# Layer 0 of a four-layer convolution and scan network: naming ScalarE's exp-and-ln table, and one silu visit for x and z

## The chip, the cores and the metric

The kernel runs on one core of a Trainium2 chip. The metric is device microseconds (us) for one execution of the whole program. A core has five engines that run side by side, each through its own queue in order: TensorE (PE, matrix products), VectorE (DVE), ScalarE (ACT, activation functions), GpSimd (POOL) and SyncE (SP, which here issues the DMA transfers).

ScalarE computes an activation function from a table that must be loaded first. `Silu`, `Exp` and `Ln` do not all lie in one table, so the program holds table loads (`ACT_TABLE_LOAD` in the profile) among ScalarE's work.

## The reference

Four layers run one after the other on an input of 2 x 128 channels x 64 x 64. Only layer 0 is touched. It is a layer norm over the channels, then a Mamba block run in four directions over the 4096 positions (rows forward and backward, columns forward and backward), then a projection of the four results and a residual sum. Cut to what matters:

```python
xz = x @ W_in.T
xh, z = split(xz, 2)
xc = causal_conv(xh, conv_w, width=4) + conv_b
xh = silu(xc)
dt, Bm, Cm = split(xh @ W_xp.T)
dt = softplus(dt @ W_dt.T + b_dt)          # exp and ln
dA = exp(dt[..., None] * A)                # A = -exp(A_log), 16 states
dBu = dt[..., None] * Bm * xh[..., None]
h = scan(h = dA * h + dBu)                 # along the positions
y = sum_over_states(h * Cm) + xh * Dp
y = y * silu(z)
return y @ W_out.T
```

The softplus is computed as `max(p, 0) + ln(1 + exp(-|p|))`, so layer 0 needs silu, exp and ln.

## The kernel before, in words

Layer 0 works through 64 chunks of 512 positions: two batch items, two orders (rows, columns), two directions (`rev` false, then true), and eight chunks in each. A chunk has 256 inner channels times 16 states, which are 32 groups of 128 rows. Two groups share one pass, so a chunk has **16 steps**, and step `s` of a chunk contains scan `s` on VectorE.

For one step, ScalarE makes `da = exp(dt * A)` into PSUM (`s_da`, line 396, two halves of 512 columns), GpSimd makes `dbu` (`s_dbu`, line 383), ScalarE corrects one column of `dbu` for the state carried over from the chunk before (`s_fix`, line 411), VectorE scans (`s_scan`, line 427), and the result is multiplied by C on VectorE (`s_hc`, line 439) or, in 5 of 16 steps, on GpSimd (line 437). TensorE sums the states (`s_y`, line 450). There are two `da` buffers in PSUM and three `dbu` buffers. So `da` of step s+1 waits for scan s-1, and `dbu` of step s+2 waits for scan s-1.

Everything is in an order written out by hand (`manual_schedule`): the loop from line 611 issues, in each step `s`, `s_dbu` of step s+2, scan `s`, VectorE's extra work `V[s]`, `s_hc` of step s-1, GpSimd's extra work `G[s]`, the sums `s_y` that are due, `s_da`, `s_fix` of step s+1 and `s_hst` of step s-1 on ScalarE, ScalarE's extra work `A[s]`, and TensorE's extra work `M[s]`. The dictionaries `A`, `V`, `M`, `G` prepare the next two chunks, `new` (the next) and `nxt` (the one after it):

- softplus for `new`: `M[0]`, `M[1]` and `A[1]`, `A[2]` (abs, `e_exp`, line 350), `A[3]` (`e_ln`, line 353), `V[5]`, `V[6]` (`dt_`, line 359), then `G[7]`, `G[8]` (`dtu_`, line 367).
- z for `new`, in the forward directions only: `pz(0)` and `pz(1)` on TensorE (line 294), each copied out by ScalarE with `z_` (line 300). They stand at `M[6]`, `A[7]` and `M[13]`, `A[14]`. `zsilu` (line 308) takes silu of both halves and stores the gate to DRAM, at `A[8]` of the chunk itself. The backward directions load the stored gate instead (`zload`).
- x for `nxt`: `px(0)` and `px(1)` (line 281, four products each) at `M[9]` and `M[10]`, copied out with `x_` (line 290) at `A[10]` and `A[12]`, then `xsilu` (line 304) at `A[13]`, `pd` (line 320) at `M[15]`.
- the layer norm of later positions in 12 chunks (`Norm0`; 0 to 3 and 15 to 22): `center` at `M[12]`, `sub` at `V[13]` (line 214), `square` at `A[14]`, `var` at `M[14]`; in the chunk after that `ln` and `exp` at `A[3]` (lines 232 and 235), `scale` at `M[7]`, `mul` at `V[8]`.

All the small products `pt`, `pz`, `px`, `pd`, `center`, `scale`, `var` and `po` pass through one PSUM buffer named `misc`. Each therefore waits until the engine that reads the one before it is done.

## Time and profile before

| what | value |
|---|---|
| three timed runs | 6545.72, 6548.74, 6561.89 us; median 6548.74 |
| profiled execution, first to last instruction (span) | 6564.3 us; no other time of that execution is recorded |
| first to last scan of layer 0 | 57.4 to 3464.2 us, 64 chunks, 53.2 us a chunk |
| busy over the span | PE 5817.9, DVE 5628.5, POOL 5420.7, ACT 4487.8 us |
| `ACT_TABLE_LOAD` | 1283 ns each |

The page prints the engines' busy shares, the span in 40 slices, the chain of work that ended last, and the costliest groups of instructions. In a line of the trace's timeline the columns are the start (us), the duration (us), the engine, the line of the kernel, the operation, what is written and read with shapes, the number of instructions merged into the row, and in brackets the idle time of the engine before it and what ended that idle time. Instructions of one engine overlap a little at their ends, so busy times are unions of intervals.

### The profile page before, as it was taken

How to read it: one execution, taken by the hardware profiler on the slowest of the kernel's cores; microseconds unless marked ns; L12 is line 12 of the kernel's file. 1: busy time of each engine (PE TensorE's matmuls, PEld its weight loads, DVE VectorE, ACT ScalarE, POOL GpSimd, SP SyncE). 2: the span in 40 equal slices, each digit the busy share in tenths (PEclk: the TensorE clock that was granted, in tenths of full speed). 3: DMA queues.
4: the chain of work that ended last, by engine and by line, in shares of the span. 5: the costliest groups of instructions: out<-in, count | busy, mean ns of one | idle time of the engine just before them, and what ended most of it. 6: DMA issues, size and time to landing. Idle time of an engine off the chain costs nothing. (4 is left out here: it accounts for less than half of the span.)

```text
span 6564.3 us, 66618 instructions
## 1 busy us (share of the span) xinstructions
PE 5817.9 (89%) x20014; PEld 2781.5 (42%) x20014; DVE 5628.5 (86%) x4540; ACT 4487.8 (68%) x7771; POOL 5420.7 (83%) x2543
## 2 busy tenths in 40 slices
PE   8888888888888888888888999999999999898888
PEld 2222222222222222222226888888888788222221
DVE  7999999999999999999997766666666766899997
ACT  7887778877788777887766665555556565555453
POOL 6999999999999999999995666655666566788886
PEclk7888777877788777887779999999999999889897
DMA  6566656566666666556650000000000000877775
GB/s 181 145 156 161 161 142 146 146 150 148 152 155 151 153 152 152 146 146 152 151 137 19 2 4 3 1 1 1 1 1 1 2 6 7 205 173 179 181 180 121
DMA packets 400476, 700.36 MB, mean 107 GB/s; under 512 B 74089, under 2 KB 76658, under 8 KB 399730
## 3 DMA queue, kind: packets, MB, share of 16 engines
q1 hardware_dynamic: 399232, 694.33, 43.3%
q8 instruction: 157, 2.57, 0.2%
q14 instruction: 205, 1.68, 0.1%
q10 hardware_dynamic: 882, 1.78, 0.1%
HBM read 584.53 MB, written 111.28 MB: 106 GB/s over the span
## 5 line engine op out<-in xcount | busy, mean ns | idle before, releaser
L383 POOL TENSOR_TENSOR dbu<-dus,bs 128x1024 f32<-128x1024 f32 x1024 | 2448.1, 2440 | 116.9 <-DVE h L427 98.8
L427 DVE TENSOR_TENSOR_SCAN h<-da,hst,dbu 128x1024 f32<-128x1024 f32 x896 | 2090.9, 2340 | 86.1 <-ACT dbu L411 80.7
L396 ACT ACTIVATE da<-dts,aneg 128x512 f32<-128x512 f32 (+1 forms) x2048 | 1410.1, 689 | 357.1 <-DVE h L427 318.9
L1004 POOL TENSOR_TENSOR sum<-sum,sc 128x1024 f32<-128x1024 f32 x378 | 898.1, 2376 | 504.1 <-ACT sc L999 500.4
L966 ACT COPY sc<-s 128x512 f32<-128x512 f32 x1024 | 596.9, 585 | 767.8 <-PE s L961 639.2
L961 PE MATMUL s<-q,k 128*128 128x256 f32 x4096 | 1053.8, 380 | 9.7 <-ACT lo L919 5.5
L1016 PE MATMUL av<-sc,v 128*128 128x256 f32 x4096 | 1051.2, 380 | 9.1 <-ACT sc L999 9.1
L450 PE MATMUL y<-hc,cst 128*32 128x512 f32 x4096 | 880.4, 753 | 200.2 <-DVE hc L439 186.6
L973 DVE TENSOR_TENSOR mx<-mx,s 128x512 f32<-128x512 f32 x896 | 609.3, 680 | 452.5 <-ACT sc L966 449.2
L439 DVE TENSOR_TENSOR hc<-h,pc 128x1024 f32<-128x1024 f32 x704 | 841.9, 1196 | 9.5 <-PE y L450 7.4
L961 PEld LDWEIGHTS s<-q,k 128*128 128x128 f32 x4096 | 777.0, 191 | 126.9 <-issue 8.8
L1016 PEld LDWEIGHTS av<-sc,v 128*128 128x128 f32 x4096 | 768.0, 190 | 112.9 <-ACT sc L999 14.1
L437 POOL TENSOR_TENSOR hc<-h,cs 128x1024 f32<-128x1024 f32 x320 | 770.0, 2406 | 1.2 <-issue 1.2
L416 PE MATMUL pc<-xd,sel 16*128 16x512 f32 x1024 | 707.0, 780 | 0.2
L1407 POOL TENSOR_TENSOR A<-A,D 128x1024 f32<-128x1024 f32 x224 | 526.9, 2370 | 138.8 <-DVE D L1412 102.1
L996 DVE TENSOR_TENSOR sc<-sc,pm 128x1024 f32<-128x1024 f32 x512 | 620.5, 1212 | 0.9 <-PE pm L992 0.9
L999 ACT ACTIVATE sc<-sc 128x1024 f32<-128x1024 f32 x512 | 541.8, 1058 | 41.2 <-DVE sc L996 41.0
L450 PEld LDWEIGHTS y<-hc,cst 128*32 128x32 f32 x4096 | 125.9, 120 | 858.3 <-DVE hc L439 427.6
L340 PE MATMUL misc<-xd,w_dt 9*128 9x512 f32 x504 | 364.6, 810 | 128.1 <-ACT x L479 68.5
L411 ACT ACTIVATE dbu<-hst,dbu,df 128x1 f32<-128x1 f32 x896 | 337.6, 377 | 65.3 <-POOL dbu L383 42.7
L1424 PE MATMUL q<-xs,room 32*128 32x512 f32 x840 | 291.1, 706 | 63.1 <-DVE A L1430 62.1
L416 PEld LDWEIGHTS pc<-xd,sel 16*128 16x128 f32 x1024 | 181.6, 218 | 350.2 <-issue 296.8
(315 smaller groups left out, 7792.9 us busy)
## 6 DMA issues: line engine op xcount, KB each, us to landing
dts<-ddt SPq DMA_DIRECT2D x512, 256.0 KB, 5.4
dus<-ddu SPq DMA_DIRECT2D x512, 256.0 KB, 5.1
D<-rows SPq DMA_DIRECT2D x448, 256.0 KB, 6.0
bs<-rows SPq DMA_DIRECT2D x1024, 64.0 KB, 4.9
cs<-rows SPq DMA_DIRECT2D x1024, 64.0 KB, 3.2
ddt<-dt SPq DMA_DIRECT2D x128, 256.0 KB, 2.0
ddu<-dtu SPq DMA_DIRECT2D x128, 256.0 KB, 4.0
dtr<-ddt SPq DMA_DIRECT2D x448, 64.0 KB, 2.0
```

Of the source, the lines that this page charges most:

```text
L383: nc.gpsimd.tensor_mul(t, self.dus[q], _bc(self.bs[g], 1, [P, 2, T]))
L396: act(t[:, i, sl], self.dts[q][:, i, sl], AF.Exp, scale=an[:, g, 2 * q + i : 2 * q + i + 1])
L416: mm(t, lhsT=sel[32:48, 4 * g : 4 * g + 4, :].rearrange("p n d -> p (n d)"), rhs=self.xd[32:48, :], start=True, stop=True)
L427: nc.vector.tensor_tensor_scan(ho, ai, bi, init, ALU.mult, ALU.add)
L437: nc.gpsimd.tensor_mul(t, self.h[u], _bc(self.cs[gq(u)[0]], 1, [P, 2, T]))
L439: nc.vector.tensor_mul(t, self.h[u], _bc(self.pc[u // 2], 1, [P, 2, T]))
L450: mm(self.y[q // 2][r : r + 32, :], lhsT=sum4, rhs=self.hc[u][:, i, :], start=False, stop=(u % 8 >= 6), skip_group_check=True)
L961: mm(p[:, o, :], lhsT=j.k[m // 8][:, m % 8 * P : m % 8 * P + P], rhs=self.q, start=True, stop=True)
L973: nc.vector.tensor_max(self.mx, self.s[0][:, 0:2, :] if u == 1 else self.mx, self.p[u])
L996: nc.vector.tensor_sub(s, s, _bc(self.pm[:, :], 1, [P, 4, NQ]))
L1004: self.adds.tensor_add(self.sum, self.s[0] if w == 1 else self.sum, self.s[w])
L1016: mm(self.av, lhsT=self.job.v[m // 8][:, m % 8, :], rhs=self.s[u // 2][:, m % 4, :], start=(m == 0), stop=(m == 31))
```

## The change

`exp_and_ln` names the table that has both `Exp` and `Ln` and loads it. It is called right behind each silu visit and ahead of the first softplus. The silu of z moves from `A[8]` of the chunk itself to `A[13]` of the chunk before it, beside the silu of x for the chunk after, so that both stand between one load of silu's table and one load of the other. Only the very first chunk keeps its z visit at `A[8]`. So that z is ready by then, its second half moves from `M[13]`, `A[14]` to `M[8]`, `A[9]`.

```diff
+    def exp_and_ln():
+        nc.scalar.preload_act_table_set("natural_log_exp_and_others")
@@ before the first softplus, and behind the second silu of x, ahead of the loop
+            exp_and_ln()
             c.e_exp()
             c.e_ln()
...
+            exp_and_ln()
             c.s_da(0)
@@ in the loop over chunks
                 if c.rev:
                     A[4] = (*A[4], c.zload)
-                else:
-                    A[8] = (c.zsilu,)
+                elif old is None:
+                    A[8] = (c.zsilu, exp_and_ln)
...
                     if not new.rev:
                         M[6], A[7] = lambda: new.pz(0), (lambda: new.z_(0),)
-                        M[13], A[14] = lambda: new.pz(1), (lambda: new.z_(1),)
+                        M[8], A[9] = lambda: new.pz(1), (lambda: new.z_(1),)
...
-                    A[13] = (nxt.xsilu,)
+                    A[13] = (nxt.xsilu, *(() if new.rev else (new.zsilu,)), exp_and_ln)
```

In the built program the list of ScalarE's instructions holds 391 table loads before the change and 202 after it; no other instruction of the program is added or dropped.

## The prediction

> **What bounds the kernel now.** I looked first at the busy times between the first and the last scan of layer 0 (time, PE, PE's weight loads, DVE, ACT, POOL, clock granted to TensorE, DMA share, GB/s).

> ```profile
> 57.40:3464.20 3406.80, 2890.37 (x7790) 791.01 (x7790) 3274.67 (x2005) 2741.65 (x5240) 3301.18 (x1469) 0.79 0.61 150
> ```

> DVE is idle for 3406.8 - 3274.7 = 132 us and POOL for 106 us. ACT, from which the change takes work, is free for 665 us. So this stage is set by DVE and POOL, and a table load counts only where it makes one of them wait. Next, the waits (total, times, longest) of DVE and of POOL:

> ```profile
> DVE h L427 <- ACT dbu L411: 80.7, 122, 1.9
> POOL dbu L383 <- DVE h L427: 98.8, 108, 1.5
> ```

> All that ACT's lateness costs DVE's scans is 80.7 us, and that caps the gain. Then the table loads (count, busy us, mean ns, idle before):

> ```profile
> L396 ACT ACT_TABLE_LOAD x146 | 187.3, 1283 | 2.7
> L353 ACT ACT_TABLE_LOAD x64 | 82.1, 1283 | 0.4
> L304 ACT ACT_TABLE_LOAD x62 | 79.5, 1283 | 0.4
> ```

> Sorting the 1024 scans by start, 16 to a chunk, I split DVE's idle time by step. Of 136 us: step 0 13.5, step 1 16.4, step 5 28.6, step 10 4.2, step 13 20.4, step 15 46.3, all others 6.8. The timeline of a forward chunk shows why. First ACT around the logarithm, `A[3]`:

> ```profile
> 2046.09 0.39 ACT L411 ACTIVATE dbu<-hst,dbu,df 128x1 f32<-128x1 f32 x1 [0.85 <-POOL dbu L383]
> 2046.57 1.28 ACT L353 ACT_TABLE_LOAD   x1
> 2047.86 1.06 ACT L353 ACTIVATE e<-e 128x1024 f32<-128x1024 f32 x1
> 2048.93 1.28 ACT L396 ACT_TABLE_LOAD   x1
> 2050.23 1.42 ACT L396 ACTIVATE da<-dts,aneg 128x512 f32<-128x512 f32 x2
> ```

> Then ACT around the silu of x, `A[13]`, in the chunk before it:

> ```profile
> 2023.92 0.69 ACT L290 ACTIVATE xs<-misc,vec 128x512 f32<-128x512 f32 x1 [0.45 <-PE y L443]
> 2024.89 1.42 ACT L396 ACTIVATE da<-dts,aneg 128x512 f32<-128x512 f32 x2 [0.28 <-DVE h L427]
> 2026.70 1.28 ACT L304 ACT_TABLE_LOAD   x1
> 2027.99 1.16 ACT L304 ACTIVATE xs<-xs 128x512 f32<-128x512 f32 x2
> ...
> 2030.46 1.42 ACT L396 ACTIVATE da<-dts,aneg 128x512 f32<-128x512 f32 x2
> ```

> And the scans they delay, 15, 0 and 5:

> ```profile
> 2032.22 2.35 DVE L427 TENSOR_TENSOR_SCAN h<-da,hst,dbu 128x1024 f32<-128x1024 f32 x1 [0.64 <-ACT dbu L411]
> 2034.80 2.35 DVE L427 TENSOR_TENSOR_SCAN h<-da,hst,dbu 128x1024 f32<-128x1024 f32 x1 [0.23 <-ACT dbu L411]
> 2051.99 2.35 DVE L427 TENSOR_TENSOR_SCAN h<-da,hst,dbu 128x1024 f32<-128x1024 f32 x1 [0.77 <-ACT dbu L411]
> ```

> In a chunk that also prepares a layer norm, the subtraction waits for TensorE:

> ```profile
> 1177.40 0.69 DVE L214 TENSOR_TENSOR xc<-x,misc 128x512 f32<-128x512 f32 x1 [1.03 <-PE misc L210]
> ```

> TensorE's rows matter since z's second product moves:

> ```profile
> 2006.07 2.08 PE L294 MATMUL misc<-xn,m 128*128 128x512 f32 x2 [1.29 <-DVE dt L359]
> 2010.07 4.64 PE L450 MATMUL y<-hc,cst 128*32 128x512 f32 x16
> 2014.64 3.70 PE L281 MATMUL misc<-xn,wk 128*128 128x512 f32 x8
> 2025.86 1.13 PE L294 MATMUL misc<-xn,m 128*128 128x512 f32 x2
> ```

> From 2006 to 2024 TensorE has no pause, and the same product took 2.08 us at 2006 and 1.13 at 2026.

> **The change part by part.** I count in DVE's time, because a chunk lasts DVE's work plus DVE's idle time. The 64 chunks fall into 11 forward ones with a layer norm in step 13 ("norm": 0 to 3, 16 to 22), 17 forward ones without ("plain": 4 to 6, 32 to 38, 48 to 54), three backward ones whose next is forward (15, 31, 47), four forward ones whose next is backward, and 29 other backward ones.

> *The loads.* The built program has 189 fewer; at 1.283 us that is 242.5 us of ACT. Almost all of it lies beside other engines' work. [...]

> *The logarithm.* Both loads at `A[3]` go, 2 x 1.29 = 2.58 us of the path from line 411 to scan 5. Scan 5 waited 0.77 us here, so the rest of the gain has no taker: without the loads `da` and its correction would be done by 2049.4, DVE is free at 2051.2. Over all chunks step 5's wait is 28.6 us: 24.0 for line 411, and 4.5 for `misc` (line 340), which is late because the copy `xo` stands behind the same loads. Gain **-28.6**. What is late next is POOL, which now waits 1.33 us at step 5 and then less; its work is 3301 / 64 = 51.6 us a chunk and stays under DVE's.

> *The z visit at `A[8]`.* Two loads and one silu (3.6 us) leave step 8. Step 10 waited 4.2 us over all chunks: **-4.2**.

> *The joint visit at `A[13]`.* It holds one more activation, 1.06 us (line 308, 33.8 us / 32), in 31 chunks. In plain and backward chunks scan 15 already waits, so all of it lands on DVE: 20 x 1.06 = **+21.2**. In norm chunks scan 15 does not wait; at 1182.17 its correction ends 0.33 us before the scan starts, so 0.73 is left: 11 x 0.73 = **+8.0**. Behind the visit ACT's queue holds `da` of steps 15 and 0. But z's copy (0.58 us) has left `A[14]`, and scan 15 is now later than `da` of step 0, so scan 0's wait of 0.23 in plain chunks goes: 3.7 us in 17 chunks, **-3.7**. In norm chunks `square` stays in that place and step 0 keeps its wait.

> *z's second product at `M[8]`.* It stands ahead of `px(0)` in a stretch where TensorE has no pause: `px(0)`, `px(1)`, the copies `x_`, and in norm chunks `center`, all move by its length d, less what it covers. No row shows it there. Below, 0: it runs while line 450 waits for its `hc`. Above, 2.07, the slow row. Between: in the plain chunk the second pair of line 450 waits for DVE until 2012.8, and starts of products are 0.85 apart until 2014.6 and 0.43 after. Put in at 2011.8, the product ends at 2013.8, the pair takes 0.85 + 0.43, and `px(0)` starts at 2015.1, d = 0.48. In the norm chunk, put in at 1163.45 with the clock rising at 1164.3, d = 0.8. In norm chunks `sub` waits for it in full: 11 x 0.8 = **+8.8**. In plain ones x's copy could be 0.18 us later before it holds up `da` of step 14 (0.35 us between the copy's end and the scan's at 2024.85, less the 0.17 that step 10 gives back): 17 x 0.30 = **+5.1**. The added wait of `z_(1)` at `A[9]` holds `da` of step 11 behind it until about 1165.6 in a norm chunk; its scan starts at 1171.8, so that is covered.

> [...]

> *The gate's store on SP's queue* moves from 2013.8 to ahead of a `dus` load issued at 2029.8, and waits for silu until about 2030.2. The loads behind come some 0.9 us later. The tightest is the last `bs`, issued by 2038.8 and landing 4.9 later; POOL takes it up at 2048.4. Nothing.

> Sum: -28.6 - 4.2 - 3.7 + 21.2 + 8.0 + 8.8 + 5.1 = **+6.6 us**. The profiled span of 6564.3 becomes 6570.9. It lies 15.6 us above the median of the runs, so I put the difference on the median: 6548.7 + 6.6 = **6555**. Bounds by d: at 0, -7.3 (6541). At 2.07, 11 x 2.07 + 17 x 1.89 in place of 13.9: +47.6 (6596).

> **The rivals.**

> *Slower: x's products come late.* With d on the slow row TensorE holds back `px`, the copies and `center`: 6596. For it: TensorE has no pause there, and 1.03 us of DVE's wait in norm chunks already hang on that chain. [...] Above 0.18 the sum is -10.4 + 28 d, so it leaves the no-change band at d = 1.07.

> *Faster: POOL keeps the beat.* POOL waits about 1.33 us, nearly the same, at step 5 of most chunks, as if the loads were a detour in its cycle and DVE's other stalls were slack. Then the 53 chunks outside the norm ones lose all of POOL's idle time (74.9 us) and the joint visit costs only the norm chunks, 16.8: 6549 - 58 = 6491. Against: a plain chunk has 51.0 us of DVE work ((898.8 - 31.4) / 17) and will have at least 1.7 us of stall at scan 15, more than POOL's 51.6. Half of it, in the backward chunks, would still be 6520.

> *The change does not do what it says*: a load comes back before an `Exp`, as 1.28 us in a place that has cover or not. The program's list speaks against it. 6549 to 6575.

> **How the numbers follow.** What can be told from no change is 0.3%, 20 us; the three runs span 16. Chances: forecast 0.50, slower rival 0.33, POOL's beat 0.14, the last 0.03. The forecast's own range is 6535 to 6575 (d from 0 to 1.1, and some 5 us of run to run). The range reaches to 6518, which takes in half of POOL's beat, and to 6597, the slow row. Part of the forecast's cases ends outside the band, more of them above: faster 0.17, same 0.46, slower 0.37.

> **What would show each step.** No table load between lines 350 and 353's `Ln` and `da`, and step 5 without a wait of scans (right: below 4 us in all). Step 15's wait up from 46 to about 75 us. `sub`'s wait in norm chunks from 1.03 to about 1.8 us, and `px(0)` 0.5 to 0.8 us later behind `dt_(1)` than before. POOL's 1.33 at step 5 turned into smaller waits at steps 3 to 5. I am wrong if step 15's wait does not grow, if `px` slips by over 1 us, or if a wait appears at a step that has none now.

## The result, and the profile after

The change made the kernel slower: 6574.41 us (median of 4 runs, 6571.81 to 6587.68) against 6550.14 us before; ratio 1.0041, 95% interval [1.0027, 1.0055]. The medians differ by 24 us; the ratio stands for 27. The profiled execution took 6587.68 us with a span of 6585.9, which is 21.6 more than the span before.

The busy times between the first and the last scan of layer 0 (time, PE, PE's weight loads, DVE, ACT, POOL, clock granted to TensorE, DMA share, GB/s), and VectorE's largest waits (total, times, longest), of the profile after. The first scan starts at 55.74 us here:

```profile
55.74:3489.10 3433.36, 2857.70 (x7789) 786.12 (x7790) 3271.98 (x2005) 2505.24 (x5051) 3301.80 (x1469) 0.78 0.61 149
```

```profile
DVE h L430 <- ACT dbu L414: 69.1, 66, 2.2
...
DVE dt L460 <- PE y L453: 30.8, 13, 2.6
DVE xc L217 <- PE misc L213: 18.7, 11, 2.0
```

ScalarE's busy time fell by 236 us (2741.65 to 2505.24); 188 of the 189 loads that are gone lie in this stretch, and at 1.283 us they make 241. VectorE's work is within 3 us of before. Yet the layer takes 26.6 us longer (3433.4 less 3406.8). The 122 waits of scans for ScalarE (80.7 us) became 66 longer ones (69.1 us), and waits for TensorE grew. By step, VectorE's idle time went from 136.2 to 166.7 us; step 0 counts the 4.1 and 5.3 us ahead of the very first scan, which is why the prediction's rows give 132 and its steps 136:

| step | 0 | 1 | 5 | 10 | 11 | 13 | 15 | others |
|---|---|---|---|---|---|---|---|---|
| before, us | 13.5 | 16.4 | 28.6 | 4.2 | 1.6 | 20.4 | 46.3 | 5.2 |
| after, us | 9.3 | 34.6 | 0.0 | 0.0 | 9.2 | 37.9 | 70.2 | 5.5 |

By kind of chunk, in sums over the chunk lengths:

| chunks | before, us | after, us | difference |
|---|---|---|---|
| 11 norm | 601.3 | 632.2 | +30.9 |
| 17 plain | 898.8 | 902.4 | +3.6 |
| 3 backward, next forward | 155.0 | 161.5 | +6.5 |
| 4 forward, next backward | 214.2 | 210.9 | -3.3 |
| 29 other backward | 1537.4 | 1526.3 | -11.1 |

The loss sits in the norm chunks. VectorE's waits in one of them, from the timeline after:

```profile
1192.38 1.22 DVE L442 TENSOR_TENSOR hc<-h,pc 128x1024 f32<-128x1024 f32 x1 [0.37 <-PE pc L419]
...
1199.97 0.69 DVE L217 TENSOR_TENSOR xc<-x,misc 128x512 f32<-128x512 f32 x1 [1.65 <-PE misc L213]
...
1205.72 2.35 DVE L430 TENSOR_TENSOR_SCAN h<-da,hst,dbu 128x1024 f32<-128x1024 f32 x1 [0.56 <-ACT dbu L414]
...
1216.65 0.69 DVE L460 TENSOR_TENSOR dt<-sz,y 128x512 f32<-128x512 f32 x1 [2.60 <-PE y L453]
```

These are the product with C at step 11, the layer norm's subtraction at step 13, scan 15, and the gating product `yg` at step 1 of the next chunk. The last was 0.90 us before:

```profile
1191.93 0.69 DVE L457 TENSOR_TENSOR dt<-sz,y 128x512 f32<-128x512 f32 x1 [0.90 <-PE y L450]
```

TensorE in the same chunk, after:

```profile
1176.24 2.08 PE L297 MATMUL misc<-xnt,m 128*128 128x512 f32 x2 [2.17 <-DVE dt L362]
...
1184.86 1.80 PE L297 MATMUL misc<-xnt,m 128*128 128x512 f32 x2
...
1187.59 3.70 PE L284 MATMUL misc<-xnt,wk 128*128 128x512 f32 x8
...
1206.35 1.87 PE L226 MATMUL misc<-meanw,sq 128*128 128x1 f32 x8 [4.38 <-ACT sq L221]
1208.15 1.93 PE L453 MATMUL y<-hc,cst 128*32 128x512 f32 x8
1210.01 3.68 PE L323 MATMUL misc<-xs,m 128*73 128x512 f32 x4
```

The same place before the change:

```profile
1154.99 2.08 PE L294 MATMUL misc<-xnt,m 128*128 128x512 f32 x2 [1.90 <-DVE dt L359]
...
1165.01 3.70 PE L281 MATMUL misc<-xnt,wk 128*128 128x512 f32 x8
...
1183.32 1.05 PE L223 MATMUL misc<-meanw,sq 128*128 128x1 f32 x8 [2.01 <-ACT sq L218]
1184.30 1.17 PE L450 MATMUL y<-hc,cst 128*32 128x512 f32 x8
```

z's second product took 1.80 us in its new place, 1.39 us of it at a granted clock of 0.50 (until 1186.25), where it took 1.13 at 1178.14 before, at 1.00; and `px(0)` starts 11.35 us behind z's first product where it started 10.02 behind it before (1165.01 less 1154.99). Then TensorE waits 4.38 us for `square` ahead of the layer norm's variance, where it waited 2.01. Counted from the start of the layer norm's subtraction, TensorE runs out of work 2.0 us later instead of 3.9, because z's product has left this place, and `square` starts 5.7 us later instead of 5.2. So most of the longer pause comes from the product that moved, and 0.5 us from the longer visit. The variance and the sums of step 15 now run at a granted clock of 0.50 (from 1203.32 to 1213.56) and take 1.87 and 1.93 us instead of 1.05 and 1.17, and the sums that `yg` needs stand behind them.

### The profile page after: what moved, and what is told of

It reads as the page before. It is cut to its first block, busy times and chain, and to the rows that moved or that the text cites. A ratio compares the mean times of both kernels' runs of the same rounds, so it can differ in the third digit from the quotient of the medians.

```text
span 6585.9 us, 66433 instructions
## 1 busy us (share of the span) xinstructions
PE 5774.6 (88%) x20014; PEld 2771.7 (42%) x20014; DVE 5626.7 (85%) x4540; ACT 4249.9 (65%) x7582; POOL 5420.0 (82%) x2543
## 5 line engine op out<-in xcount | busy, mean ns | idle before, releaser
L430 DVE TENSOR_TENSOR_SCAN h<-da,hst,dbu 128x1024 f32<-128x1024 f32 x896 | 2088.9, 2339 | 83.6 <-ACT dbu L414 69.1
L419 PE MATMUL pc<-xd,sel 16*128 16x512 f32 x1024 | 687.1, 758 | 1.3
L343 PE MATMUL misc<-xd,w_dt 9*128 9x512 f32 x504 | 338.6, 756 | 139.4 <-DVE dt L362 108.6
```

What stands on the lines that cost most here:

```text
L419: mm(t, lhsT=sel[32:48, 4 * g : 4 * g + 4, :].rearrange("p n d -> p (n d)"), rhs=self.xd[32:48, :], start=True, stop=True)
L430: nc.vector.tensor_tensor_scan(ho, ai, bi, init, ALU.mult, ALU.add)
```

## The experiments

**The naming alone.**

```diff
     A[8] = (c.zsilu, exp_and_ln)          # in every forward chunk
     M[13], A[14] = lambda: new.pz(1), (lambda: new.z_(1),)
     A[13] = (nxt.xsilu, exp_and_ln)
```

> Only the naming: each silu visit keeps its old place, and the table with exp and ln is loaded behind it, so the two loads around the logarithm (and the one before the layer norm's exp) go, and nothing else moves. Theory A (what I now hold: the stalls at step 5 were real losses of VectorE, the rest of the change costs more than that): step 5's idle time of VectorE falls from 28.6 us to under 4, no other step's grows by more than 5 us in all, and the time is 22 to 33 us under before, about 6522. Rival B (GpSimd keeps the beat): the 1.33 us a chunk that it waits go as well, 60 us or more under before, 6490. Rival C (freed time comes back as another wait, such as TensorE's slow clock before px): within 8 us of before.

Measured: 6524.18 us, ratio 0.9959 [0.9947, 0.9972], faster than both kernels. Step 5's wait is 0 and no other step's grew by more than some 3 us. The norm chunks stayed at 601.0 us, and the plain ones fell to 888.1. Theory A holds: the waits at step 5 were real, and no more than them was to be had. GpSimd still idles 80 us in layer 0 (105 before), so rival B falls. VectorE's waits for ScalarE in this run:

```profile
DVE h L430 <- ACT dbu L414: 56.1, 90, 1.9
```

**The joint visit without the norm chunks.**

```diff
+    joint = not new.rev and ln is None
-    A[13] = (nxt.xsilu, *(() if new.rev else (new.zsilu,)), exp_and_ln)
+    A[13] = (nxt.xsilu, *((new.zsilu,) if joint else ()), exp_and_ln)
```

> The change, but in the 12 chunks that centre a layer norm z's second product, its copy and z's silu keep their old places (step 13, step 14, and step 8 of the next chunk). Theory A (the layer norm's chunks carry the loss: they went from 54.7 to 57.5 us): those chunks return to about 54.5 us, and the time falls by 27 to 34 us against the change, to about 6543. Rival D (the longer visit costs alike in all forward chunks): the time falls by no more than 12 us, to 6562 or above.

Measured: 6545.02 us, ratio 0.9993 [0.9982, 1.0003], 29 us less than the change. The norm chunks are back at 602.2 us, so theory A holds. Against the naming alone the joint visit in the other forward chunks still costs: the plain chunks take 903.7 us where the naming alone has 888.1, 0.92 us a chunk.

**Filling TensorE's pause.**

```diff
+    def fill(c_=new):
+        mm(misc(), lhsT=w_zT[:, P:], rhs=c_.src[:, c_.t0 + 3 : c_.t0 + 3 + T],
+           start=True, stop=True)
+    M[13] = fill
```

> The change plus one more z product, whose result nobody reads, in step 13 of the chunks that centre a layer norm, where the second z product stood before: it fills 1.1 us of TensorE's pause of 4.4 us ahead of the variance (2.0 us before the change). Theory E (the pause is long enough for TensorE's clock to drop, which makes the variance, the sums and pd slow and yg late): step 1's wait of VectorE in these chunks falls from 2.6 us to between 0.9 and 1.7, and the time falls by 8 to 18 us against the change, to about 6562. Rival F (yg is late because square itself is late behind the visit): step 1's wait stays at 2.4 us or more, and the time within 4 us of the change.

Measured: 6574.43 us, the same as the change, though step 1's wait fell as theory E said. TensorE's pause is 2.46 us here, and the variance takes 1.05 us again in the chunk shown:

```profile
1211.47 0.69 DVE L460 TENSOR_TENSOR dt<-sz,y 128x512 f32<-128x512 f32 x1 [0.75 <-PE y L453]
...
1246.32 1.22 DVE L442 TENSOR_TENSOR hc<-h,pc 128x1024 f32<-128x1024 f32 x1 [1.42 <-PE pc L419]
...
1253.91 0.69 DVE L217 TENSOR_TENSOR xc<-x,misc 128x512 f32<-128x512 f32 x1 [1.65 <-PE misc L213]
```

Step 1's wait fell from 24.5 to 13.6 us over the 11 norm chunks, and step 11's rose from 5.1 to 11.9. Both theories miss: the pause does make `yg` late, as E says, but 6.8 of the 10.9 us gained there are lost again at step 11, and the run's time does not fall. Chunks 18 to 22 take 57.90, 57.90, 57.85, 57.28 and 57.63 us, so their length doesn't settle.

**Without z's activation.**

```diff
-                act(self.sz, self.sz, AF.Silu)
+                if self.b == 0 and self.order == 0 and self.first:
+                    act(self.sz, self.sz, AF.Silu)
```

> The change without the activation that takes silu of z, in all chunks but the first: the gate is z itself, the loads, copies and products stay. It prices the 1.06 us that the joint visit adds. Theory A: step 15's wait falls by about 1.06 us in the 20 chunks without a layer norm, and by 0.56 in the others, where the variance also comes 1.06 us earlier and TensorE's pause shortens to about 3.3 us: together 27 to 42 us against the change, about 6540. Rival G (what costs is z's second product at step 8): 15 us or less, 6560 or above.

Measured: 6557.77 us, 16.6 less than the change, which lies between theory A (27 to 42) and rival G (15 or less). In plain chunks step 15's wait fell from 31.8 to 16.2 us (0.92 a chunk), of which 5 us came back at step 1. In norm chunks it fell to 0, and yet their length stayed: 58.03 us in the settled ones, which are the last of chunks 16 to 22, where the length no longer changes. A norm chunk of this run:

```profile
1212.44 0.69 DVE L461 TENSOR_TENSOR dt<-sz,y 128x512 f32<-128x512 f32 x1 [2.15 <-PE y L454]
...
1247.58 1.22 DVE L443 TENSOR_TENSOR hc<-h,pc 128x1024 f32<-128x1024 f32 x1 [1.71 <-PE pc L420]
...
1255.18 0.69 DVE L217 TENSOR_TENSOR xc<-x,misc 128x512 f32<-128x512 f32 x1 [1.65 <-PE misc L213]
```

So z's second product in its new place is enough for the loss there, and a wait that is taken away returns at another step (step 11, 5.1 to 15.6 us). That asked for what holds the length.

**A chunk in whole clock windows.** The granted clock, laid over one norm chunk before the change (columns: stretch, length, PE busy, granted clock, DMA share, GB/s):

```profile
1130.52:1133.93 3.41, 3.33 (x8) 0.50 1.09 221
1133.93:1140.76 6.83, 5.70 (x19) 1.00 0.69 147
1140.76:1144.17 3.41, 3.41 (x5) 0.50 0.00 0
1144.17:1151.00 6.83, 5.43 (x23) 1.00 0.00 1
1151.00:1164.65 13.65, 11.07 (x29) 0.50 0.48 131
1164.65:1185.13 20.48, 17.69 (x64) 1.00 0.87 216
```

And after it:

```profile
1155.53:1158.94 3.41, 3.34 (x15) 1.00 1.06 233
1158.94:1165.77 6.83, 6.16 (x10) 0.50 0.09 23
1165.77:1172.60 6.83, 5.04 (x25) 1.00 0.00 0
1172.60:1186.25 13.65, 10.81 (x20) 0.50 0.52 137
1186.25:1203.32 17.07, 15.73 (x51) 1.00 0.62 152
1203.32:1213.56 10.24, 7.21 (x20) 0.50 1.04 241
```

The clock records of these two traces hold 372 stretches before and 384 after, each granted at 0.50 or 1.00. All but the last of each trace, where the record ends, are whole multiples of 3.413 us; a "window" stands for that length here. The stretches of one turn are 1 + 2 + 1 + 2 + 4 + 6 = 16 before, 1 + 2 + 2 + 4 + 5 + 3 = 17 after. Over consecutive settled norm chunks the pattern repeats exactly (four times from 1075.90 to 1294.36 before, six times from 971.21 to 1319.37 after), and the chunk's length is the pattern's: 54.61 and 58.03 us. TensorE's pause ahead of the variance shows in it too. Before the change the clock falls behind that pause, for one window (the stretch at 1130.52); after it the clock falls inside the pause, at 1203.32, and stays low for three. The chunk lengths (chunks 18 to 22, from the scans):

```text
before                       54.91 54.54 54.60 54.60 54.61
after                        58.25 58.14 58.09 58.06 58.03
naming alone                 54.79 54.66 54.62 54.62 54.62
without z's activation       57.77 57.97 58.00 58.03 58.02
```

Three runs put work of other sizes, or in other places, into the norm chunks of the naming alone.

```diff
+    def more_work():                       # e6: range(1), e7: range(3)
+        for _ in range(1):
+            nc.vector.tensor_mul(scr, scr, scr)
+    V[3] = more_work
```

> The naming alone (6524 us) plus one product of 128x512 on VectorE (some 0.6 us) behind scan 3 in the 12 chunks that centre a layer norm. TensorE's granted clock changes only at multiples of 3.413 us, and in a row of such chunks its pattern repeats after 16 of these windows (54.61 us, which is the chunk's length) before the change and after 17 (58.03 us) with it. Theory H (the chunk is locked to a whole number of clock windows, and its stalls take up what is left): its length stays at 54.61 us, less idle time on VectorE making room, or goes to 58.03. Rival I (work simply adds up): 55.2 us.

Measured: 6565.07 us, ratio 0.9999 [0.9985, 1.0013] to the kernel before on that chip, where the naming alone has 0.9959. Settled norm chunks take 58.03 us. The product takes 0.67 us there, and in four of the unsettled chunks 4.2 to 5.3 us. The waits of a settled chunk for TensorE, with the added product:

```profile
1220.54 0.69 DVE L462 TENSOR_TENSOR dt<-sz,y 128x512 f32<-128x512 f32 x1 [2.35 <-PE y L455]
...
1226.78 0.67 DVE L663 TENSOR_TENSOR scr<-scr 128x512 f32<-128x512 f32 x1
...
1255.01 1.22 DVE L444 TENSOR_TENSOR hc<-h,pc 128x1024 f32<-128x1024 f32 x1 [0.43 <-PE pc L421]
...
1262.60 0.69 DVE L219 TENSOR_TENSOR xc<-x,misc 128x512 f32<-128x512 f32 x1 [1.65 <-PE misc L215]
```

In the naming alone these waits are:

```profile
1239.59 0.69 DVE L460 TENSOR_TENSOR dt<-sz,y 128x512 f32<-128x512 f32 x1 [0.90 <-PE y L453]
...
1279.68 0.69 DVE L217 TENSOR_TENSOR xc<-x,misc 128x512 f32<-128x512 f32 x1 [1.04 <-PE misc L213]
```

Work of 0.67 us went with a chunk that is 3.41 us longer, and the waits at steps 1, 11 and 13 are close to those of the change, with neither the joint visit nor the early product in the kernel. The GpSimd product that starts beside it took 2.80 us, where the naming alone has 2.41. One rival is left untested: that the long products in the first chunks pushed the loop into the longer pattern, and that it would have stayed there without the short ones.

> The same with three products behind scan 3 (some 1.9 us). Theory H (a whole number of clock windows): 58.03 us, so about 3.4 us more in each of the 8 settled chunks, or still 54.61. Rival I (work adds up): 56.5 us.

Measured: 6603.27 us, ratio 1.0060 [1.0038, 1.0082], and 61.44 us in the settled chunks, which is 18 windows. The expectation missed the number: the second of the three products took 2.8 us there, so the added work is about 4.2 us and not 1.9. By adding up, the chunk would take some 58.8 us.

```diff
+    extra = [lambda: act(scr, scr, AF.Silu)] * 2 if ln is not None else []
-    A[13] = (nxt.xsilu, exp_and_ln)
+    A[13] = (nxt.xsilu, *extra, exp_and_ln)
```

> The naming alone plus two unread silu activations of 128x512 (1.15 us) in the visit of step 13, only in the 12 chunks that centre a layer norm: the longer visit without z's early product. My prediction's sum (0.73 us a chunk): 55.3 us a chunk, 8 us in all. Theory H (whole clock windows): 54.61 or 58.03. If 58.03, the longer visit alone is enough for the loss; if 54.61 or 55.3, z's early product is needed for it (the run without z's activation stayed at 58.0 with the early product).

Measured: 6565.98 us, ratio 0.9997 [0.9983, 1.0011], and 58.03 us in the settled chunks. Step 15's wait is 0.80 us, close to what my sum has for a visit that much longer; the chunk grew by 3.41 us, one window, so 2.6 us are not in that sum. So the longer visit alone is enough too. Theory H holds in the settled chunks of all three: 54.61, 58.03, 61.44, and no length between. It has limits. The run that filled TensorE's pause did not settle (57.28 to 57.90 us), and plain chunks are not held to whole windows: in the second run of the naming alone 9 of the 17 take 52.01 us, which is 15.2 windows.

**Silu of x straight from PSUM.**

```diff
-                act(self.xs[i], self.px_, AF.Identity, bias=v(f"cb{i}"))
+                act(self.xs[i], self.px_, AF.Silu, bias=v(f"cb{i}"))
+                exp_and_ln()
-                    A[13] = (nxt.xsilu, exp_and_ln)
```

> The naming, with silu of x taken straight out of PSUM in x_ (steps 10 and 12) in place of a copy there and a visit at step 13: each of the two has a load of silu's table, which can run while ScalarE waits for TensorE, and a load back. 124 more loads than the naming alone, 124 silu activations fewer. Theory A (VectorE's wait at step 15, 44 us, comes from the visit's length between da of step 14 and of step 15): step 15's wait falls under 10 us, the time by 20 to 40 us against the naming alone, 6484 to 6504. Rival J (more loads cost more: da of steps 12 and 14 come 1.3 us later and the waits move to steps 12 and 14): no gain or a loss.

Measured: 6609.94 us, ratio 1.0067 [1.0048, 1.0087]. Step 15's wait is gone, but steps 12 and 14 wait 51 and 56 us, and step 1 62. Scans' waits for ScalarE in this run:

```profile
DVE h L431 <- ACT hst L436: 125.4, 115, 2.0
...
DVE h L431 <- ACT dbu L415: 23.1, 47, 1.9
DVE h L431 <- ACT da L400: 15.2, 13, 2.4
```

This is rival J's result: steps 12 and 14, where the added loads stand, now wait. J says nothing of step 1. There 43 of the 62 us stand in the 29 backward chunks, 10 of which take 54.6 to 54.7 us, again 16 windows; how much of this run's loss is the loads and how much the windows stays open.

**TensorE kept busy in backward chunks.**

```diff
+    def fill():
+        mm(misc()[:, :256], lhsT=w_zT[:, 0:P], rhs=xn[:, 3:259], start=True, stop=True)
+    if warm:                               # c.rev, no layer norm
+        M[8] = fill
...
     cy.s_y(u)
+    if warm and s == 9:
+        fill()
     cy.s_y(u + 1)
```

> The naming alone plus two unread products of 256 columns on TensorE in 26 backward chunks, in its two pauses of 1.2 and 1.4 us ahead of px(0) (between the sums of step 8 and those of steps 6 and 7's groups). In these chunks px(0) starts at the slow clock in every second chunk, and VectorE then waits at steps 11 to 13: 14 us in the 29 backward chunks, and two chunks in a row take 105.8 us, which is 31 clock windows. Theory K (the pauses let the clock drop): these waits fall under 4 us, and the time 8 to 14 us under the naming alone. Rival L (another wait holds the pair of chunks at 31 windows): within 5 us of the naming alone. Rival M (the added products delay px(0) by their own 1 us each): slower than the naming alone.

> The naming alone again, beside the run above on the same chip: 0.996 of before, as the first time, if that gain does not hang on the chip.

Measured on one chip: 0.9949 [0.9933, 0.9964] with the products, 0.9950 [0.9936, 0.9964] for the naming alone, so its gain holds on another chip, and the products' own gain does not show in the runs. In the profiled executions the waits at steps 11 to 13 of the backward chunks fell from 13.1 us to 0, step 15's by another 14 us, and these chunks from 1527.7 to 1505.9. But step 1's wait rose by 9 us, and the three chunks ahead of a forward one took 9.1 more. Theory K is right as to the waits: the mean granted clock in the backward chunks rose from 0.78 to 0.83. By the ratios of the runs rival L holds. Whether the 12.7 us that layer 0 took less in that one profile are worth anything in general stays open.

## Why the prediction was right or wrong, point by point

The range held the time, but the likeliest case, no change at +6.6 us, is not what came: measured are 24 to 27 us, about 0.4%. The range reached that far because of the slower rival, and what happened is only in part what that rival says. In layer 0 the sum misses by 20 us (26.6 less 6.6), and 15.6 of them stand in the norm chunks.

- **The loads** lie beside other work: right. 236 us left ScalarE and none of it showed by itself.
- **The logarithm**, -28.6: right. Step 5 is at 0.0, and the naming alone gained 25 us. GpSimd's beat was refuted by the same run, which should then have gained 60.
- **The z visit at step 8**, -4.2, and **scan 0 in plain chunks**, -3.7: right (4.2 to 0, and 3.7 to 0.3 us).
- **The joint visit in plain chunks.** Their step 15 went from 11.1 to 31.8 us, +20.7, where the prediction had 18.0 and 5.1 for the late `px`, 23.1: right within 3 us. (One reading there is off: by its own row x's copy ends at 2024.61, 0.24 us ahead of the scan's end and not 0.35, which would have made the 5.1 a 7.0.)

```profile
2011.41 4.59 DVE L430 TENSOR_TENSOR_SCAN h<-da,hst,dbu 128x1024 f32<-128x1024 f32 x2 [1.58 <-ACT dbu L414]
...
2064.70 4.59 DVE L430 TENSOR_TENSOR_SCAN h<-da,hst,dbu 128x1024 f32<-128x1024 f32 x2 [2.21 <-ACT dbu L414]
```

These are scans 15 of two plain chunks in a row after the change, 1.58 and 2.21 us; before, 0.64.

- **The 29 backward chunks**: step 5 there was worth 12.9, and they gained 11.1. **The three ahead of a forward chunk** lost 6.5 where the sum had 2.8: their wait is 8.5 us at step 13 for GpSimd's product (line 440), not at step 15. Why it stands there was not tried; the run with TensorE kept busy has this wait too (2.0 to 2.8 us a chunk), without the joint visit.
- **The norm chunks: the step that failed.** The prediction put 8.0 us on the longer visit and 8.8 on d, said that step 0 keeps its wait, and had no term for step 1. The two priced terms came out near: scan 15 waits 5.3 us in these chunks for 8.0, and the waits at steps 11 to 13 rose by 12.9 for 8.8, d being 1.33 and not 0.8 us (the clock rose at 1164.65 in the chunk that the prediction read, not at 1164.3). Two of the prediction's own signs of being wrong came with this: `px` slipped by over 1 us, and step 11 waits in these chunks, where it had no wait. What was left out is step 1, +12.7 us. `square` now comes behind the longer visit and z's product no longer stands in TensorE's pause ahead of it, so the pause is 4.38 us, the clock is at half for three windows instead of one, and `yg` waits. And the sum as such does not apply there: 54.61 + 1.4 us is no length at which such a chunk settled. It settled at the next whole number of windows. The settled chunks grew by 3.42 us for 1.4, and all eleven by 30.9 us where the prediction's terms leave 15.3 (16.8 less 1.5 at step 5). That accounts for most of the miss.
- **The slower rival** named `px` running late at the slow clock, with d = 2.07. The product was slow (1.80 us, the clock at 0.50 until 1186.25), but the waits at steps 11 to 13 that hang on it are 12.9 of the 30.9 us; the rest was lost behind it, mainly at step 1 and step 15. The lower bound, d = 0, did not come either: d was 1.33 us in the norm chunks. What the sum lacked is the length at which a norm chunk settles, a whole number of 3.413 us.

## What to carry to other kernels

Remove a table load where an engine waits for its end, and leave the rest where it has cover: here the naming alone gives 0.9959 and 0.9950 of before, the joint visit takes it all back and more. Before adding up microseconds in a loop, lay the granted clock over some turns of it: if turns settle at a whole number of clock windows, as the norm chunks do here, a small addition can cost a whole window (3.41 us for 0.67), and a stall that is removed can come back elsewhere. A product moved away from one of TensorE's pauses can cost more than its own time: here the pause that it left grew from 2.01 to 4.38 us, the granted clock fell from 1.00 to 0.50 inside it, and with the product (1.80 us) in its new place the settled chunks took 3.42 us more than before, in the run without z's activation too.
